# Two dense banks for the second unit's scores in a paired visit of a two-layer graph attention kernel

## The chip, the cores and the metric

The kernel runs on one core of one Trainium2 chip. The metric is the device time of one execution in microseconds (us), the median of several runs. The profile shows one more execution, instruction by instruction: TensorE's matmuls (PE) and its weight loads (PEld), VectorE (DVE), ScalarE (ACT), GpSimd (POOL), and SyncE (SP), which here issues the transfers.

## The reference, cut to what matters

There are 64 graphs of 256 nodes with 512 features, and an adjacency mask of 256 x 256 for each. Two attention layers follow each other:

```python
h = relu(layernorm(x))
x = x + attention0(h, adj)          # 4 heads of 64; masked scores, softmax, values, output product
h = relu(layernorm(x))
x = x + attention1(h, adj)          # LayerNorm with gamma and beta, 8 heads of 64; mask = adj | eye
```

In each layer q, k and v are products of h with weights. For each head the scores q k^T are scaled, masked and passed through a softmax; the probabilities weigh v; the heads together are multiplied with an output weight and added to x. Everything is fp32.

## The kernel before, in words

**Tiling.** A step works on two graphs (G = 2), so there are 32 steps. Heads are taken in pairs of two 64-row halves; a pair with its two graphs is called a *unit*. Layer 0 has the units 0 and 1, layer 1 has 0 to 3. Scores are held with keys on the partitions, so the sum over keys is a small matmul with ones.

**Dense products.** Each dense product (`project_qk`, `project_v1`, `combine`) is made of seven block products, a *set*, in the order 1, 6, 5, 2, 7, 3, 4 (the output product of layer 1 has 1, 5, 2, 6, 7, 3, 4). Products 2, 3 and 4 are accumulated into the PSUM bank that 1, 5 and 7 have left, so these banks are held between the two. One such product of the projections takes about 1.75 us on TensorE (56 passes of a set in 12.2 us). Sums of input blocks (`act_sums0`, `act_sums1`) are made on POOL ahead of a set, sums of weight blocks by `weight_sum`.

**PSUM.** Of eight banks, four are the pool `ps_sc` for scores and for the weighed values, taken in rotation. Four are `ps_mm` with the names m0 to m3; `mm_tile` takes the first bank of the list `banks` that is not held, and moves it to the end of the list.

**Visits.** Between the sets stand *visits* (`visit`). A paired visit finishes two units of an earlier attention and starts two of the next:

- `key_sums`: sums of the probabilities over keys, for both old units, into one dense bank (L961)
- `invert`: the reciprocal of the sums in two halves (L983), a check of their extremes (L986), and eight transfers by SP that spread the result (L995)
- `weigh_out`: values weighed by probabilities (L931), into two banks of `ps_sc`, copied out by ACT (L943)
- `scores` for each new unit (L875): four banks, one for each graph g and each head half e
- `mask_scores` (L899, DVE): adds the mask, reading one score bank each
- `exponentials` (L904, ACT), `key_halves` (L908, POOL), and `normalise` (L1000, POOL), which multiplies the old units' values with the spread reciprocals

With two new units there are ten tiles of the four `ps_sc` banks in one visit: two for weighed values, four for the first unit, four for the second.

**What sets the order.** Nothing is scheduled by the compiler on PE, DVE, ACT and POOL: every step is entered with a place in a period (`at`, `at_dense`, `at_set`), the entries are sorted by place, and that is the order on each engine. Period units are about the length of a set on TensorE, 7 products. In the steady part there are three paired visits in a period: at AT_X = 2.0 ahead of the v products of layer 1, at AT_Q0 = 4.64 ahead of the q and k products of layer 0, and at AT_Z = 6.36 ahead of the q and k products of layer 1. An engine works through its own order strictly, and waits at each instruction for what it needs.

**The start.** The weights of layer 1 come transposed. `weight_load(n)` loads a quarter, `weight_block` transposes one of 16 blocks on TensorE (L466) into a dense bank and copies it out in two halves (L471), on DVE or ACT. In this part `combine_rows` (L849) makes the output product of layer 0 for the first graphs in four rows, each evacuated by DVE (L854) and put through two rounds of statistics (L577, L578), POOL (L587 and around it) and ACT (L593), before `transpose_h` (L662).

Of the kernel before, what the change touches and what calls it, by code (L numbers as in the profile page):

```python
# [8 lines left out]
FP = mybir.dt.float32  # L9
# [306 lines left out]
def fast_path(  # L316
# [19 lines left out]
    nc = tc.nc  # L336
    P = 128
    B, N, D = x.shape
    DH = 64
    G = 2  # L340
    NSTEP = B // G
    NIC = N // P
# [14 lines left out]
    ps_sc = ctx.enter_context(tc.tile_pool(name="ps_sc", bufs=4, space=bass.MemoryType.PSUM))  # L357
# [4 lines left out]
    banks, held = ["m0", "m1", "m2", "m3"], set()  # L362

    def mm_tile(shape, dt=FP, hold=False):
        tag = next(b for b in banks if b not in held)
        banks.remove(tag)
        banks.append(tag)
        if hold:
            held.add(tag)
        return ps_mm.tile(shape, dt, name="mm", tag=tag)  # L370
# [82 lines left out]
    def weight_load(n):  # L453

        if n == 1:
            wr = io.tile([P, 4, D], FP, name="wr", tag="xt")
        else:
            wr = act.tile([P, 4, D], FP, name="wr", tag="v1")
        src, r0 = (w_qkv, 4 * n) if n < 3 else (w_out, 0)
        nc.sync.dma_start(wr, src[r0 * P:(r0 + 4) * P].rearrange("(r p) i -> p r i", p=P))  # L460
        return wr

    def weight_block(wr, n, c):
        pw = mm_tile([P, 4 * P])
        for r in range(4):
            nc.tensor.transpose(pw[:, r * P:(r + 1) * P], wr[:, r, c * P:(c + 1) * P], ident)  # L466
        for i in range(2):
            blk = A_OF[i, c // HC]
            dst = wqkv1[:, blk, c % HC, n, :] if n < 3 else wo1[:, blk, c % HC, :]
            copy = nc.vector.tensor_copy if i == 0 and (n > 1 or c == 0) else nc.scalar.copy  # L470
            copy(dst, pw[:, i * H1:(i + 1) * H1])  # L471


# [387 lines left out]

    units = [0]

    def scores(s, lyr, pr):
        st = S[s]
        qk = st.pop(("qk", lyr, pr))
        sc = [[ps_sc.tile([P, NIC, N], FP, name="sc") for e in range(2)] for g in range(G)]
        for g in range(G):  # L870
            for kc in range(NIC):
                for e in range(2):
                    rows = slice(e * DH, (e + 1) * DH)
                    k0 = g * N + kc * P
                    nc.tensor.matmul(  # L875
                        sc[g][e][:, kc, :], qk[rows, 1, k0:k0 + P],
                        qk[rows, 0, g * N:(g + 1) * N], start=True, stop=True,
                    )

        last = (s, lyr) == (NSTEP - 1, 1)  # L880
        if last and pr == 1:
            both = act.tile([P, 2, G, NIC, N], FP, name="p", tag="h")
            p = [both[:, e] for e in range(2)]
        elif last and pr == 3:
            p = [
                wqk0[:, 4:6].rearrange("p n c k o -> p (n c k o)").rearrange("p (g k n) -> p g k n", g=G, k=NIC),
                act.tile([P, G, NIC, N], FP, name="p", tag="v0"),
            ]
        else:
            p = [sm.tile([P, G, NIC, N], FP, name="p", bufs=4) for _ in range(2)]  # L890
        pd = sm.tile([P, 2, G, N], FP, name="pd", bufs=2)
        st["sc", lyr, pr], st["p", lyr, pr] = sc, (p, pd)
# [58 lines left out]
    def key_sums(s, lyr, prs):  # L951

        st = S[s]
        bank = mm_tile([P, 2, N])
        for i, pr in enumerate(prs):
            _, pd = st["p", lyr, pr]
            st["sums", lyr, pr] = bank[:, i]
            for g in range(G):
                for e in range(2):
                    r0 = 32 * (2 * g + e)  # L960
                    nc.tensor.matmul(  # L961
                        bank[r0:r0 + 32, i, :], ones, pd[:, e, g, :], start=True, stop=True,
                        skip_group_check=True,
                    )
# [41 lines left out]
    PERIOD, FIRST = 6.4, 6.2  # L1006
# [3 lines left out]
    def at(period, place, fn, *args):  # L1010
        events.append((period * (PERIOD if period >= 0 else FIRST) + place, len(events), fn, args))
# [15 lines left out]
    def visit(period, w, prev, cur):  # L1027

        w -= 0.0003
        s, lyr, prs = prev  # L1030
        last = (s, lyr) == (NSTEP - 1, 1)
        if prs:
            at(period, w, key_sums, s, lyr, prs)
            if prs[0] == 0 and not last:
                at(period, w, place_values, s, lyr)
            for i, pr in enumerate(prs):
                k = i if len(prs) > 1 else pr % 2
                at(period, w + 0.1 * last, invert, s, lyr, pr, k, (0,) if i and not last else (0, 1))
                if not last:
                    at(period, w, weigh_out, s, lyr, pr)  # L1040
                    at(period, w + (0.55 if len(prs) == 1 else (0.3, 0.75)[i]), normalise, s, lyr, pr)
        for i, pr in enumerate(cur[2]):
            unit = (*cur[:2], pr)
            one = len(cur[2]) == 1
            at(period, w, scores, *unit)
            at(period, w, mask_scores, *unit, 0)
            at(period, w + 1 / 7 if one else w, mask_scores, *unit, 1)
            if i == 0 and len(prs) > 1 and not last:
                at(period, w, invert, s, lyr, prs[1], 1, (1,))
            for g, place in enumerate((0.05, 0.22) if one else ((0.02, 0.03), (0.15, 0.3))[i]):  # L1050
                at(period, w + place, exponentials, *unit, g)
            for e, place in enumerate((0.23, 0.3) if one else ((0.1, 0.11), (0.35, 0.36))[i]):
                at(period, w + place, key_halves, *unit, e)

    AT_X, AT_C0, AT_Q0, AT_V0, AT_H1, AT_Z = 2.0, 4.0, 4.64, 5.64, 6.21, 6.36
    LAST_QK = 4.0
    none, L0, L1A, L1B = (NSTEP, 0, ()), (0, 1), (0, 2), (1, 3)
    for s in range(NSTEP - 1):
        visit(s, AT_X, (s + 1, 0, L0), (s, 1, L1A))
        if s < NSTEP - 2:  # L1060
            visit(s, AT_Q0, (s, 1, L1A), (s, 1, L1B))
            visit(s, AT_Z, (s, 1, L1B), (s + 2, 0, L0))

    p = NSTEP - 2
# [10 lines left out]
    visit(-2, FIRST_V0, none, (0, 0, (0,)))  # L1075
    visit(-2, FIRST_H1, (0, 0, (0,)), (0, 0, (1,)))
    visit(-2, FIRST_H1 + 0.67, (0, 0, (1,)), none)
    visit(-1, 1.53, none, (1, 0, L0))
    for s in range(NSTEP):

        p = s - 2
# [30 lines left out]
        for t in range(NT):  # L1112
            place = (FIRST_V0 + 0.14 * t - (0 if t else 0.0005), (4.31, 5.02, 5.16, 5.31)[t])[s] if s < 2 else AT_V0 + 0.14 * t
            at_dense(p, place, 0.14, project_v0, s, t)
        p = s - 1
        if s == 0:
            p -= 2.23 / FIRST
        edge = 0 if s == 0 else 1 if s == NSTEP - 1 else 2
# [12 lines left out]
        for k in range(NT):  # L1131
# [6 lines left out]
            place = ((3.6112, 3.6113, 3.7502, 3.7503)[k], 3.6 + 0.01 * k, 5.85 + 0.06 * k)[edge]  # L1138
            at(p, place, scale_row, s, NORM1[k] if edge < 2 else k)

        turn = (3.765, 3.9995, AT_H1)[edge]
        for c in range(NC):
            at(p, turn + 0.00001 * c, transpose_h, s, 1, c)
        at(p, turn + (0.001, 0.0001, 0.155)[edge], lambda s=s: act_sums0(S[s]["hT"]))
# [1 line left out]
        p = s  # L1146
        if s < NSTEP - 1:
# [3 lines left out]
            p, place = (s + 1, 1.0) if s < NSTEP - 2 else (s, LAST_QK + 2)  # L1151
# [4 lines left out]
        else:  # L1156
            p = s - 1
# [16 lines left out]
    for i in range(4):  # L1174
        at(-2, 3.01, weight_sum, nc.vector, wqk0, i)
        at(0, 0.9, weight_sum, nc.gpsimd, wo0, i)
    for n, (p, place) in enumerate(((-2, 4.0), (-2, 4.0), (-1, 0.0), (-1, 1.7))):
        at(p, place, lambda n=n: blocks.update({n: weight_load(n)}))
    at(-2, FIRST_V0 + 0.2, lambda: gamma_beta(gbr[0]))
    for i in range(16):  # L1180
        place = 3.3 - 3.93 + (1 + i) / 7 - 0.0005 if i < 6 else 0.3701 + 0.0001 * i if i < 8 else 1.6 + 0.01 * (i - 8) if i < 12 else 6.2 + 0.9995
        at(-1, place, lambda i=i: weight_block(blocks[i // 4], i // 4, i % 4))
    for i in range(4):
        at(-1, 0.1 + 0.01 * i, weight_sum, nc.vector, wqkv1[:, :, :, 0, :], i)
# [57 lines left out]
```

## Time and profile before

| what | value |
|---|---|
| median of three runs | 3425.72 us (3424.96 to 3425.89) |
| the profiled execution | 3424.34 us, span 3422.6 us |
| granted TensorE clock | 0.999 |
| PE busy | 3403.6 us, 99% of the span |
| POOL, DVE, ACT busy | 65%, 57%, 37% |
| scores, L875: matmuls | 3072 passes, 462.9 us busy |
| scores, L875: weight loads | 314.7 us busy, 151.3 us idle before them |
| one steady period (between the visits at 1483.41 and 1589.34 us) | 105.9 us |

Busy time of matmuls includes their overlap: they are pipelined, and a pass of 256 columns is shown with about 380 ns though one starts every 0.216 us. So a short stall between two passes does not show as idle time of PE. It shows as idle time ahead of a weight load (PEld), and in the distance from one matmul's start to the next. Each matmul of fp32 appears as two passes in the trace: the eight matmuls of a unit's scores are 16 passes.

### The profile page before, as it was taken

Reading aid. Unit: us, or ns where it says so; the run is one execution under the profiler, and the core shown is the slowest. Engines: PE = TensorE matmul, PEld = TensorE weight load, DVE = VectorE, ACT = ScalarE, POOL = GpSimd, SP = SyncE. Lnnn points to the kernel's source line nnn. Section 1 sums busy time; section 2 is a strip of 40 time slices with the busy share of each in tenths; the row PEclk is TensorE's granted clock in tenths of the full one; section 3 lists DMA queues with packets and bytes.
Section 4 is the critical chain, followed back from the end, with each engine's and each line's share of the span. In section 5 each row is a group of like instructions: output and inputs, shape, how many; then the busy total and the mean of one; then the engine's idle time right before and its main releaser. Section 6 shows DMA issues by size and latency. Waiting matters only on the chain.

```text
span 3422.6 us, 59964 instructions
## 1 busy us (share of the span) xinstructions
PE 3403.6 (99%) x22962; PEld 2741.9 (80%) x22962; DVE 1960.1 (57%) x3445; ACT 1253.6 (37%) x2221; POOL 2239.5 (65%) x2124
## 2 busy tenths in 40 slices
PE   9999999999999999999999999999999999999999
PEld 6878788787888878788787888888787887878877
DVE  6555655556555565555655555555556555565555
ACT  4334343333433333433434234343343433334331
POOL 6867675666766666666666576666676766667653
PEclk9999999999999999999999999999999999999999
DMA  4112111211111120111211112111111112111111
GB/s 129 42 56 59 44 43 42 58 57 50 38 54 48 55 61 27 56 46 55 61 30 55 44 55 61 35 52 42 57 59 45 43 42 58 57 52 35 55 31 45
DMA packets 168132, 174.08 MB, mean 51 GB/s; under 512 B 59672, under 2 KB 113056, under 8 KB 167840
## 3 DMA queue, kind: packets, MB, share of 16 engines
q1 hardware_dynamic: 167408, 169.78, 16.9%
q8 instruction: 184, 3.01, 0.4%
q14 instruction: 108, 0.88, 0.1%
q10 hardware_dynamic: 432, 0.40, 0.0%
HBM read 86.12 MB, written 33.62 MB: 35 GB/s over the span
## 4 chain that ended last, share of the span: by engine, by line
PE 85%; POOL 13%; issue 1%; DVE 1%; DMA 1%; SPq 0%; ACT 0%; POOLq 0%
PE mm L766 33%; PE mm L823 17%; PE sc L875 12%; PE mm L807 12%; PE sc L931 7%; POOL xt L639 4%; POOL qk L776 2%; PE mm L961 2%; PE mm L662 2%; POOL hT L412 1%; POOL hT L409 1%; POOL hT L413 1%; POOL n L569 1%; POOL r L587 1%; POOL n L572 1%
## 5 line engine op out<-in xcount | busy, mean ns | idle before, releaser
L908 POOL TENSOR_TENSOR pd<-p 128x512 f32<-128x512 f32 x383 | 478.1, 1269 | 494.1 <-ACT p L904 492.5
L766 PE MATMUL mm<-hT,wqkv 128*128 128x256 f32 x3584 | 787.4, 380 | 1.0 <-ACT wqkv L471 1.0
L766 PEld LDWEIGHTS mm<-hT,wqkv 128*128 128x128 f32 x3584 | 678.2, 190 | 103.2 <-issue 11.1
L823 PE MATMUL mm<-wo,oT 128*128 128x256 f32 x2632 | 585.6, 380 | 0.4
L823 PEld LDWEIGHTS mm<-wo,oT 128*128 128x128 f32 x2632 | 495.1, 190 | 77.1 <-POOL hT L414 11.1
L899 DVE TENSOR_TENSOR p<-sc,n 128x512 f32<-128x512 f32 x766 | 475.0, 682 | 110.5 <-PE sc L875 109.1
L983 DVE RECIPROCAL oT<-mm 128x128 f32<-128x128 f32 x376 | 345.1, 939 | 290.0 <-PE mm L961 286.3
L904 ACT ACTIVATE p<-p 128x512 f32<-128x512 f32 x766 | 443.6, 627 | 174.9 <-DVE p L899 174.5
L875 PE MATMUL sc<-qk 64*128 64x256 f32 x3072 | 462.9, 402 | 2.3
L875 PEld LDWEIGHTS sc<-qk 64*128 64x128 f32 x3072 | 314.7, 186 | 151.3 <-DVE p L899 75.9
L807 PE MATMUL mm<-wqkv,hT 128*128 128x256 f32 x1792 | 401.9, 382 | 0.0
L766 PE MATMUL mm<-hT,wqk 128*128 128x256 f32 x1792 | 399.0, 382 | 0.7 <-DVE qk L706 0.6
L943 ACT COPY oT<-sc 128x512 f32<-128x512 f32 x188 | 110.0, 585 | 762.9 <-PE sc L931 758.7
L766 PEld LDWEIGHTS mm<-hT,wqk 128*128 128x128 f32 x1792 | 338.2, 191 | 56.6 <-issue 11.3
L807 PEld LDWEIGHTS mm<-wqkv,hT 128*128 128x128 f32 x1792 | 335.5, 190 | 53.8 <-issue 10.7
L931 PE MATMUL sc<-p,v 128*32 128x256 f32 x6128 | 349.9, 379 | 0.4 <-issue 0.4
L931 PEld LDWEIGHTS sc<-p,v 128*32 128x32 f32 x6128 | 199.8, 110 | 132.2 <-issue 1.2
L1000 POOL TENSOR_TENSOR oT<-oT 128x512 f32<-128x512 f32 x188 | 239.3, 1273 | 60.3 <-DMA oT<-oT 54.0
L734 POOL TENSOR_TENSOR xt<-xt,u 128x512 f32<-128x512 f32 x183 | 229.6, 1276 | 11.4 <-DVE xt L723 9.0
L793 PE MATMUL mm<-wv,hT 128*128 128x256 f32 x1024 | 226.9, 379 | 0.0
L793 PEld LDWEIGHTS mm<-wv,hT 128*128 128x128 f32 x1024 | 194.3, 190 | 27.1 <-issue 0.6
L409 POOL TENSOR_TENSOR hT<-hT 128x512 f32<-128x512 f32 x64 | 81.7, 1277 | 185.7 <-ACT hT L666 174.6
(132 smaller groups left out, 3660.9 us busy)
## 6 DMA issues: line engine op xcount, KB each, us to landing
oT<-oT SPq DMA_DIRECT2D x1504, 32.0 KB, 1.9
xt<-in_x_dram SPq DMA_DIRECT2D x31, 1024.0 KB, 6.0
h<-in_x_dram SPq DMA_DIRECT2D x31, 1024.0 KB, 5.5
out_dram<-xt SPq DMA_DIRECT2D x31, 1024.0 KB, 4.4
ne<-row SPq DMA_DIRECT2D x30, 256.0 KB, 4.8
ad<-in_adj_dram SPq DMA_DIRECT2D x32, 128.0 KB, 9.1
wr<-in_L_gnn_w_qkv_dram SPq DMA_DIRECT2D x3, 1024.0 KB, 8.7
h<-in_x_dram SPq DMA_DIRECT2D x4, 256.0 KB, 3.9
```

The source lines that it names most:

```text
L734: (nc.vector if last else nc.gpsimd).tensor_tensor(r, r, u, ALU.add)
L766: nc.tensor.matmul(bank[:, k, :], w[:, wa, c, k, a * P:(a + 1) * P], st["hT"][:, ba, c, :], start=first and (k, c) == (0, 0), stop=(k, c) ...
L793: nc.tensor.matmul(bank, st["hT"][:, b0 + t // NIC * step, c % HC, i:i + P], wv0[:, c, :], start=(c == 0), stop=(c == NC - 1),)
L807: nc.tensor.matmul(bank[:, t, :], st["hT"][:, ba, c, t * P:(t + 1) * P], wqkv1[:, wa, c, 2, :], start=first and (t, c) == (0, 0), stop=(t, ...
L823: nc.tensor.matmul(bank[:, t, :], oT[:, ba, c, t * P:(t + 1) * P], w[:, wa, c, :], start=first and (t, c) == (0, 0), stop=(t, c) == (NIC - ...
L875: nc.tensor.matmul(sc[g][e][:, kc, :], qk[rows, 1, k0:k0 + P], qk[rows, 0, g * N:(g + 1) * N], start=True, stop=True,)
L899: nc.vector.tensor_tensor(p[e][:, g], sc[e], neg[:, :, g, :], ALU.add)
L904: nc.scalar.activation(p[e][:, g], p[e][:, g], AF.Exp, scale=SCALE)
L908: nc.gpsimd.tensor_tensor(pd[:, e], p[e][:, :, 0, :], p[e][:, :, 1, :], ALU.add)
L931: nc.tensor.matmul(po[r0:r0 + 32, g, :], st[f"v{lyr}"][:, g * NIC + kc, pr * P + r0:pr * P + r0 + 32], p[r0 // DH][:, g, kc, :], start=(kc ...
L983: nc.vector.reciprocal(inv[:, k * P:(k + 1) * P], sums[:, k * P:(k + 1) * P])
L1000: nc.gpsimd.tensor_tensor(dst, dst, invb, ALU.mult)
```

## The change

There are three edits.

First, in a paired visit the second unit's scores of the first graph (g = 0) go into two banks of `ps_mm`, taken by `mm_tile`, in place of two of `ps_sc`. The bank that holds the sums of the keys in this visit is remembered in `sums_bank`, and moved to the end of the list, so that later dense products take it last. A visit then has eight tiles of `ps_sc`: the second unit's second graph (g = 1) takes the two banks of the first unit's first graph.

Second, on DVE the second half of the second old unit's reciprocal, with its check and its transfers, moves from the place behind the first new unit's masks to a place between the second new unit's two pairs of masks.

Third, in the start: weight blocks 7 to 11 get other places (block 7 behind a v product, 8 to 11 one behind each row of `combine_rows`), the load of the last quarter is entered at 1.1 in place of 1.7, the copies of five blocks go to ACT instead of DVE, the visit for step 1 becomes two visits of one unit each, on either side of the transposes of step 0's h, and the late place of the second mask is kept for step 0 alone.

```diff
-            copy = nc.vector.tensor_copy if i == 0 and (n > 1 or c == 0) else nc.scalar.copy
+            copy = nc.vector.tensor_copy if i == 0 and (n > 2 or (n, c) == (0, 0)) else nc.scalar.copy
...
-    units = [0]
+    units, sums_bank = [0], []
-    def scores(s, lyr, pr):
+    def scores(s, lyr, pr, second):
         st = S[s]
         qk = st.pop(("qk", lyr, pr))
-        sc = [[ps_sc.tile([P, NIC, N], FP, name="sc") for e in range(2)] for g in range(G)]
+        sc = [
+            [mm_tile([P, NIC, N]) if second and g == 0 else ps_sc.tile([P, NIC, N], FP, name="sc") for e in range(2)]
+            for g in range(G)
+        ]
+        if second and sums_bank:
+            tag = sums_bank.pop()
+            banks.remove(tag)
+            banks.append(tag)
...
         bank = mm_tile([P, 2, N])
+        sums_bank[:] = [banks[-1]] if len(prs) > 1 else []
...
-            one = len(cur[2]) == 1
-            at(period, w, scores, *unit)
+            one = cur[:2] == (0, 0)
+            at(period, w, scores, *unit, i == 1)
             at(period, w, mask_scores, *unit, 0)
+            if i == 1 and len(prs) > 1 and not last:
+                at(period, w, invert, s, lyr, prs[1], 1, (1,))
             at(period, w + 1 / 7 if one else w, mask_scores, *unit, 1)
-            if i == 0 and len(prs) > 1 and not last:
-                at(period, w, invert, s, lyr, prs[1], 1, (1,))
...
-    visit(-1, 1.53, none, (1, 0, L0))
+    visit(-1, 1.53, none, (1, 0, (0,)))
+    visit(-1, 1.54, none, (1, 0, (1,)))
...
-        turn = (3.765, 3.9995, AT_H1)[edge]
+        turn = (3.763, 3.9995, AT_H1)[edge]
...
-    for n, (p, place) in enumerate(((-2, 4.0), (-2, 4.0), (-1, 0.0), (-1, 1.7))):
+    for n, (p, place) in enumerate(((-2, 4.0), (-2, 4.0), (-1, 0.0), (-1, 1.1))):
...
-        place = 3.3 - 3.93 + (1 + i) / 7 - 0.0005 if i < 6 else 0.3701 + 0.0001 * i if i < 8 else 1.6 + 0.01 * (i - 8) if i < 12 else 6.2 + 0.9995
+        place = (
+            *(3.3 - 3.93 + (1 + k) / 7 - 0.0005 for k in range(7)), 0.5205,
+            *(0.53 + 0.14 * (k + 1) - 0.0005 for k in range(4)), *(FIRST + 0.9995 for k in range(4)),
+        )[i]
```

## The prediction

> **What bounds the kernel now.** I read the page first: busy times, then the costliest groups; then the waits, and last the timeline of single visits.
>
> ```profile
> span 3422.6 us, 59964 instructions
> PE 3403.6 (99%) x22962; PEld 2741.9 (80%) x22962; DVE 1960.1 (57%) x3445; ACT 1253.6 (37%) x2221; POOL 2239.5 (65%) x2124
> ...
> L899 DVE TENSOR_TENSOR p<-sc,n 128x512 f32<-128x512 f32 x766 | 475.0, 682 | 110.5 <-PE sc L875 109.1
> ...
> L875 PE MATMUL sc<-qk 64*128 64x256 f32 x3072 | 462.9, 402 | 2.3
> L875 PEld LDWEIGHTS sc<-qk 64*128 64x128 f32 x3072 | 314.7, 186 | 151.3 <-DVE p L899 75.9 <-issue 40.3 <-POOL hT L413 13.0
> ```
>
> TensorE is busy 99% of the span, so only what shortens its own stream shortens the kernel. But its matmuls overlap, and a short stall hides inside "busy". The weight loads beside it (PEld) show it: one group, the scores of L875, has its loads idle for 151.3 us, half of that until a mask addition (L899, DVE) had read a score bank. The list of waits says the same:
>
> ```profile
> PEld sc L875 <- DVE p L899: 75.9, 254, 0.4
> ```
>
> 254 such waits over the paired visits is 2.7 each. One visit of the steady part, weight loads, then matmuls, then DVE:
>
> ```profile
> 1525.54 1.60 PEld L875 LDWEIGHTS sc<-qk 64*128 64x128 f32 x16 [0.41 <-issue]
> 1527.45 0.29 PEld L875 LDWEIGHTS sc<-qk 64*128 64x128 f32 x2 [0.31 <-DVE p L899]
> 1528.05 0.89 PEld L875 LDWEIGHTS sc<-qk 64*128 64x128 f32 x8 [0.30 <-DVE p L899]
> 1529.24 0.73 PEld L875 LDWEIGHTS sc<-qk 64*128 64x128 f32 x6 [0.30 <-DVE p L899]
> ```
> ```profile
> 1525.54 4.83 PE L875 MATMUL sc<-qk 64*128 64x256 f32 x32
> 1530.30 12.35 PE L766 MATMUL mm<-hT,wqk 128*128 128x256 f32 x56
> ```
> ```profile
> 1526.70 2.48 DVE L899 TENSOR_TENSOR p<-sc,n 128x512 f32<-128x512 f32 x4 [1.14 <-PE sc L875]
> 1529.11 0.95 DVE L983 RECIPROCAL oT<-mm 128x128 f32<-128x128 f32 x1
> ...
> 1530.43 2.48 DVE L899 TENSOR_TENSOR p<-sc,n 128x512 f32<-128x512 f32 x4
> ```
>
> The first unit's 16 passes load without a break. The second unit restarts at 1527.45, 1528.05 and 1529.24, each just after a mask ended: its four banks are the first unit's, and masks come at 0.60 us a bank. The stage costs 1530.30 - 1525.54 = 4.76 us. What would it cost unstalled? A visit of one unit shows it:
>
> ```profile
> 29.27 2.00 PE L875 MATMUL sc<-qk 64*128 64x256 f32 x16
> 31.20 1.99 PE L793 MATMUL mm<-wv,hT 128*128 128x256 f32 x8
> ```
>
> 16 passes take 31.20 - 29.27 = 1.93 us, entering and leaving the form included. Passes go in pairs (two row halves at once) every 0.216 us (inside the visit: 1526.290, 1526.506, 1526.721), so 16 more cost 8 x 0.216 = 1.73, and 32 cost 3.66. A paired visit loses 1.10 us, and 1.17 where it takes 4.83.
>
> **What the Trainium skill says.** "PSUM — Partial Sum Buffer", Specifications: eight banks a partition; four serve scores and four the dense products here, so banks can only be borrowed. "Perfetto Trace Analysis", Matmuls: independent groups should rotate through different banks, so that evacuation overlaps the next group. The trace agrees: 0.30 us idle at each restart where the second unit reuses the first one's banks, none inside the first. "TensorE: Matmul & The Clock Gate", The mechanism: matmuls start and end in program order. So a late bank holds all that follows, and any new wait of a dense product would too.
>
> **The change, part by part.** Times count from a visit's first score pass, V.
>
> 1. *Banks.* The second unit's g=0 takes two dense banks. Their last readers stand ahead of this visit's reciprocals on DVE, or ended on ACT before, so they are free. The second unit's g=1 then takes the score banks of the first unit's g=0. Unstalled it wants them at V + 0.31 + 11 x 0.216 = V+2.69, its weights some 0.19 us earlier, V+2.50. The masks freed them at 1527.45 and 1528.05, V+1.91 and V+2.51. So in the visits of 4.76 us the stall goes almost wholly. In the 4.83 us kind the second bank comes at V+2.58 (1558.27 after 1555.69), 0.08 late; I charge 0.1. Counting all 94 paired visits with an earlier pair (three in each of 30 rounds, one more in the last, three at the end) by their own durations gives 105.6 us; less 0.1 x 30, **102.6 us off TensorE's path**.
>
> 2. *The new wait.* The dense banks are now also freed by masks. The order of the set is 1, 6, 5, 2, 7, 3, 4; product 1 gets the fourth, untouched bank, products 6 and 5 the borrowed ones, 7 the bank of the sums. Product 6 starts at V+3.66+1.73 = V+5.4, 5 at V+7.1. With the masks of the second unit's g=0 ahead of the reciprocal, DVE has them done at V+3.57+0.60 = 4.2 and 4.8: 1.2 us or more to spare, cost nothing. Without that move the reciprocal (0.95), the check (0.43) and the accumulator read would stand in front, and they would end at 5.5 and 6.1, too late for 6. The sums' bank is free at about V+6.1, product 7 wants it at V+10.6. Behind product 6 on TensorE's queue is the whole set; nobody waits if it doesn't.
>
> 3. *Reciprocal later.* The second reciprocal half moves behind two masks, 1.2 us, and with it eight SP transfers (0.62 us each to issue, 1.9 to land) and one multiplication L1000 on POOL. No work is added: the second unit's last mask ends at V+7.4 as before. In the visit at 1555.69 L1000 would go from 1567.24 to about 1568.4, and the four sums of oT1 behind it on POOL from 1573.5 to 1574.7. The output product needing the second of them starts 3 x 1.75 us into the stage that began at 1572.71, or 1.17 earlier now: 1576.8 against 1572.2. Cost nothing, 4 us of cover. At most visits a DMA wait on POOL grows by about 1 us, in POOL's 35% idle time.
>
> 4. *Does the rest keep up?* After the visit at 1525.54 DVE idles 1.21 us for a dense product (1534.13), so its work moves up with TensorE; the chain from it over POOL (L587) and ACT (L593, done 1548.51) ends 0.88 us ahead of the transposes at 1549.39, and keeps that. A round is 105.9 us, with DVE at 60, POOL at 70: neither becomes the bound at 102.6.
>
> 5. *Weight blocks and the first rounds.* Same transposes, other places; five 0.42 us copies go from DVE to ACT. Two TensorE stalls there go, 0.8 us (two blocks in a row at 62.51, waiting for L710) and 1.1 us (L766 at 86.43, for L471), and 1.0 from the visit at 76.87: 4.83 against two single visits of 1.93 around the transposes. New risks: block 8 wants its rows at about 65.7 (their packets ended near 63, from 57.69); the transposes at 80.1 want rows scaled by about 79.5, since the four products of L849, spread out by blocks, still feed DVE at its own rate. On SP the output weights' load is issued before the next graph's h. Between -1 and +3 us; I take a gain of 2.5.
>
> Sum: 102.6 + 2.5 = 105.1. The profiled execution took 3424.34 us (span 3422.6), so 3319.2; the median of the runs is 1.4 higher, **3320.7 us**, 3.1% less.
>
> **The rivals.**
> - *A: as above*, 76%: 3312 to 3330, by part 5's bounds and up to 0.1 us a visit on the restart.
> - *B: the second half still restarts.* The bank needed at V+2.50 comes at V+2.51; if the wait costs a whole restart (0.31 instead of 0.216) plus lateness at each of two banks, 0.3 us a visit stay: 28 us, about 3349, or 3330 to 3360. For it: the margins are zero in 62 visits and negative in 30. Against: inside 1525.54 a load 0.015 us late shifted nothing. 15%.
> - *C: given back downstream.* TensorE arrives 1.1 us earlier at the transposes, whose rows have 0.88 us of cover, if one link stays fixed in time (ACT's exponentials move up only 0.8 us). Once a round up to 1.1 us, or two such waits: 3360 to 3415. Against: the chain's DVE part waited for TensorE. 5%.
> - *D: slower.* Product 6 waits for a borrowed bank. It decides when the mask ends past V+5.4, and turns the sum when it is over 1.1 us later still, V+6.5, against V+4.2 worked out. At 0.3 us beyond that in each visit it gives 3425.7 + 28 = 3454. It needs DVE 2.3 us late. 3%.
> - *E: nothing happens*, if the dense banks were never free at the visit; the wait would only change its name. 1%.
>
> **How the numbers follow.** About 0.2% (7 us) is what a measurement of this kernel can tell from no change. A, B and C are faster: 0.96; E is the same: 0.01; slower 0.03. The likeliest is A, 3320.7. The range runs from 3312 (A's lower end, all of the 3 us of part 5 and no restart) to 3348, to take in the larger part of B.
>
> **What would show it.** Right: the wait of L875's loads for the masks falls from 75.9 us to under 10; a paired visit lasts 3.66 to 3.8 us from its first score pass to the next product; the next products have no new idle loads; a round takes 102.4 to 102.7 us; the additions of L899 now read mm as well as sc; POOL's wait for DMA at L1000 rises from 54.0 us, at no cost. B would leave restarts in the second unit's last eight passes. C would show loads of L662 or L823 idle for ACT or POOL. D would show loads of the second product in a set idle for the mask additions. I am wrong if the visits shorten and the round doesn't.

## The result and the profile after

| | us |
|---|---|
| before, median of four runs | 3425.48 (3424.96 to 3425.89) |
| after, median | 3316.51 (3316.21 to 3317.53) |
| ratio | 0.9682 (0.9666 to 0.9699) |
| the profiled execution after | 3317.53, span 3315.7 |
| predicted | 3320.7 (3312 to 3348) |

The kernel is 109.0 us faster, 3.2%. The page of the kernel after, its busy times and the groups of the scores (now L883) and of the mask additions (now L907; the last line is from the list of groups by form):

```profile
PE 3298.3 (99%) x22962; PEld 2717.9 (82%) x22962; DVE 1959.3 (59%) x3440; ACT 1260.5 (38%) x2226; POOL 2244.7 (68%) x2124
...
L907 DVE TENSOR_TENSOR p<-sc,n 128x512 f32<-128x512 f32 x579 | 363.6, 684 | 111.2 <-PE sc L883 109.8
...
L883 PE MATMUL sc<-qk 64*128 64x256 f32 x2320 | 292.6, 385 | 0.0
L883 PEld LDWEIGHTS sc<-qk 64*128 64x128 f32 x2320 | 218.7, 186 | 58.8 <-issue 38.8
```
```profile
L907 DVE TENSOR_TENSOR p<-mm,n 128x512 f32<-128x512 f32 x187 | 119.6, 681 | 0.0
L883 PE MATMUL mm<-qk 64*128 64x256 f32 x752 | 96.8, 376 | 0.0
L883 PEld LDWEIGHTS mm<-qk 64*128 64x128 f32 x752 | 72.8, 187 | 8.3
```

The scores now stand in two groups: 752 passes, eight in each of the 94 paired visits, write mm. The idle time ahead of the loads is 58.8 + 8.3 = 67.1 us; it was 151.3. The mask additions, which ended 75.9 us of it, are gone from the list. So is a line of the kernel before that stood for the same thing:

```profile
PEld sc L875 <- POOL hT L413: 13.0, 29, 0.4
```

These 29 loads start 0.11 to 0.12 us after a mask addition has ended, at V+2.04 (V is the start of the visit's first score pass). With them and two more called "issue" there are 285 restarts, three in each of the 95 paired visits of the kernel before, where the prediction read 254, or 2.7 each. The largest part of what is left is "issue", 0.41 us once a visit where the form of the matmuls changes. TensorE issues as many passes as before, 22962; only their spacing changed.

One visit, weight loads and then DVE, of the kind shown before (it starts at 1479.36):

```profile
1479.36 1.60 PEld L883 LDWEIGHTS sc<-qk 64*128 64x128 f32 x16 [0.41 <-issue]
1480.98 0.84 PEld L883 LDWEIGHTS mm<-qk 64*128 64x128 f32 x8
1481.84 0.84 PEld L883 LDWEIGHTS sc<-qk 64*128 64x128 f32 x8
1483.02 11.95 PEld L766 LDWEIGHTS mm<-hT,wqk 128*128 128x128 f32 x56 [0.33 <-issue]
```
```profile
1480.53 2.48 DVE L907 TENSOR_TENSOR p<-sc,n 128x512 f32<-128x512 f32 x4 [1.14 <-PE sc L883]
1482.93 1.28 DVE L907 TENSOR_TENSOR p<-mm,n 128x512 f32<-128x512 f32 x2
...
1484.12 0.95 DVE L992 RECIPROCAL oT<-mm 128x128 f32<-128x128 f32 x1
...
1485.45 1.28 DVE L907 TENSOR_TENSOR p<-sc,n 128x512 f32<-128x512 f32 x2
```

The 32 passes load in one stream, and from the first to the next product it is 1483.02 - 1479.36 = 3.66 us (3.65 in the mean of all 94 visits). The 56 loads of the next set follow without a break, so no new wait stands behind it. DVE does what it did, in the new order. A round went from 105.9 to 102.55 us.

### The profile page after: what moved, and what is told of

The parts are those of the page before. It is cut to its first block, busy times and chain, and to the rows that moved or that the text cites. A ratio compares the mean times of both kernels' runs of the same rounds, so it can differ in the third digit from the quotient of the medians.

```text
span 3315.7 us, 60001 instructions
## 1 busy us (share of the span) xinstructions
PE 3298.3 (99%) x22962; PEld 2717.9 (82%) x22962; DVE 1959.3 (59%) x3440; ACT 1260.5 (38%) x2226; POOL 2244.7 (68%) x2124
## 4 chain that ended last, share of the span: by engine, by line
PE 99%; DMA 1%; DVE 0%; SPq 0%; issue 0%; DVEq 0%
PE mm L766 35%; PE mm L823 17%; PE mm L807 12%; PE sc L939 10%; PE sc L883 8%; PE mm L793 7%; PE mm L662 3%; PE mm L970 3%; PE mm L883 2%; PE mm L550 0%; PE mm L849 0%; DMA h<-in_x_dram 0%; PE mm L466 0%; DMA wv<-in_L_gnn_Wv_dram 0%; SPq L431 0%
## 5 line engine op out<-in xcount | busy, mean ns | idle before, releaser
L766 PE MATMUL mm<-hT,wqkv 128*128 128x256 f32 x3584 | 787.4, 380 | 0.0
L766 PEld LDWEIGHTS mm<-hT,wqkv 128*128 128x128 f32 x3584 | 678.2, 190 | 102.2 <-issue 11.4
L823 PE MATMUL mm<-wo,oT 128*128 128x256 f32 x2632 | 585.7, 380 | 0.4
L823 PEld LDWEIGHTS mm<-wo,oT 128*128 128x128 f32 x2632 | 495.0, 190 | 77.3 <-POOL hT L414 11.2
L907 DVE TENSOR_TENSOR p<-sc,n 128x512 f32<-128x512 f32 x579 | 363.6, 684 | 111.2 <-PE sc L883 109.8
L766 PE MATMUL mm<-hT,wqk 128*128 128x256 f32 x1792 | 398.7, 382 | 1.6 <-DVE qk L706 1.3
L766 PEld LDWEIGHTS mm<-hT,wqk 128*128 128x128 f32 x1792 | 338.2, 191 | 57.6 <-issue 12.0
L883 PE MATMUL sc<-qk 64*128 64x256 f32 x2320 | 292.6, 385 | 0.0
L883 PEld LDWEIGHTS sc<-qk 64*128 64x128 f32 x2320 | 218.7, 186 | 58.8 <-issue 38.8
L593 ACT ACTIVATE h<-h,mr,r 128x512 f32<-128x512 f32 x252 | 188.2, 809 | 16.3 <-POOL mr L589 16.3
```

Source lines behind the costliest of these rows:

```text
L766: nc.tensor.matmul(bank[:, k, :], w[:, wa, c, k, a * P:(a + 1) * P], st["hT"][:, ba, c, :], start=first and (k, c) == (0, 0), stop=(k, c) ...
L823: nc.tensor.matmul(bank[:, t, :], oT[:, ba, c, t * P:(t + 1) * P], w[:, wa, c, :], start=first and (t, c) == (0, 0), stop=(t, c) == (NIC - ...
L883: nc.tensor.matmul(sc[g][e][:, kc, :], qk[rows, 1, k0:k0 + P], qk[rows, 0, g * N:(g + 1) * N], start=True, stop=True,)
L907: nc.vector.tensor_tensor(p[e][:, g], sc[e], neg[:, :, g, :], ALU.add)
```

## The experiments

The first four share one chip and its runs of the kernel before (median 3425.07 us), the last three another (3425.08). The kernel after has no runs on these two chips, so the ratios to the kernel before are what can be compared.

**Borrowed banks with the masks in the old order.**

```diff
-            if i == 1 and len(prs) > 1 and not last:
-                at(period, w, invert, s, lyr, prs[1], 1, (1,))
             at(period, w + 1 / 7 if one else w, mask_scores, *unit, 1)
+            if i == 0 and len(prs) > 1 and not last:
+                at(period, w, invert, s, lyr, prs[1], 1, (1,))
```

> The changed kernel with the second half of the reciprocal back in its old place, ahead of the second unit's masks; the borrowed banks stay. My theory (the borrowed bank holds product 6 until its mask is done): the mask of the second unit's first bank then ends at about V+5.6 instead of V+4.3, product 6 wants its bank at V+5.2, so each of some 91 visits loses about 0.35 us: 3345 to 3353 us, with idle weight loads of the second product of a set, put down to the mask additions. Rival (the order of the masks is idle, the banks alone carry the gain): 3316 to 3319. Rival (a visit's gain depends on both in full): 3400 or more.

Measured: 3346.87 us, ratio 0.9772 (0.9755 to 0.9788): 30 us of the 109 are lost. The timeline of a visit that starts at 1449.94, DVE and the next set's loads:

```profile
1453.51 0.95 DVE L992 RECIPROCAL oT<-mm 128x128 f32<-128x128 f32 x1
1453.59 1.59 PEld L807 LDWEIGHTS mm<-wqkv,hT 128*128 128x128 f32 x8 [0.33 <-issue]
...
1454.84 1.28 DVE L907 TENSOR_TENSOR p<-mm,n 128x512 f32<-128x512 f32 x2
1455.58 1.59 PEld L807 LDWEIGHTS mm<-wqkv,hT 128*128 128x128 f32 x8 [0.39 <-DVE p L907]
```

The scores still run in 3.65 us; the stall has moved to the ninth pass of the set, where product 6 takes a bank whose mask now stands behind the reciprocal. Its loads stand idle 0.39 us, and a round has 103.52 us, 0.97 more, 0.32 a visit. So the order of the masks is worth 30 us, but only together with the banks:

**The masks' order without the banks.** The same lines moved as in the change, in the kernel before.

> The kernel before with the masks of the second unit's first graph moved ahead of the reciprocal's second half, and no borrowed banks. My theory: the second unit restarts behind the FIRST unit's masks, which don't move, so 3424 to 3427 us, the same as before, with the same 254 waits of about 0.30 us. Rival (earlier masks free banks earlier, and carry a part of the gain): 3420 or less.

Measured: 3424.74 us, ratio 0.9999 (0.9990 to 1.0007). The list of waits is what it was:

```profile
PEld sc L875 <- DVE p L899: 76.1, 254, 0.4
```

The second unit restarts behind the first unit's masks, and those don't move.

**The sums' bank left in its turn.**

```diff
-        if second and sums_bank:
+        if False:
```

> The changed kernel without the step that moves the bank of the key sums to the end of the list: product 6 then gets that bank, and waits for the check behind the second reciprocal half, which ends at about V+6.1 where the product wants the bank at V+5.2. My theory: 0.8 to 0.95 us in each of some 92 visits, 3390 to 3404 us, most of the gain gone. Rival (something in the visit is later anyway and hides it): 3316 to 3330.

Measured: 3414.79 us, ratio 0.9970 (0.9959 to 0.9982). Nearly the whole gain goes, 98 us, and more than expected. A visit that starts at 1475.20:

```profile
1480.95 0.43 DVE L995 CUSTOM_DVE_ANT_0 mm<-mm,oT 128x256 f32<-128x256 f32 x1
1481.30 0.14 DVE L995 DVE_READ_ACCUMULATOR2_ANT extremes<- 128x1 f32 x1
...
1481.49 5.04 PEld L807 LDWEIGHTS mm<-wqkv,hT 128*128 128x128 f32 x24 [1.04 <-DVE extremes L995]
```

The accumulator read ends at V+6.24 and the load starts at V+6.29, where the expectation had V+6.1. In the visits ahead of L766 the list of waits names POOL instead (69.5 us, 61 times), but there too the load that waits starts 0.11 us after the accumulator read, in nearly every visit. A round grows by 2.92 us, 0.97 a visit, and the last visit, whose reciprocals are entered later, stops TensorE once for 5.0 us. Without the three lines that put one name at the end of a list, nine tenths of the gain are gone.

**One borrowed bank.**

```diff
-            [mm_tile([P, NIC, N]) if second and g == 0 else ps_sc.tile([P, NIC, N], FP, name="sc") for e in range(2)]
+            [mm_tile([P, NIC, N]) if second and g == 0 and e == 0 else ps_sc.tile([P, NIC, N], FP, name="sc") for e in range(2)]
```

> The changed kernel with one borrowed bank instead of two (g=0, e=0 alone); the other three of the second unit stay in the score banks. My theory (each score bank of the second unit waits for the mask addition of the one it takes over): restarts of about 0.2 us at the second bank (free at V+1.9, wanted at V+1.6) and 0.3 us at the last (free at V+3.1, wanted at V+2.7): 0.5 us a visit, 3358 to 3370 us. Rival (the restart at V+1.9 alone): 3330 to 3340. Rival (no gain below two banks): 3400 or more.

Measured: 3367.12 us, ratio 0.9830 (0.9814 to 0.9847); a visit lasts 4.19 us in the mean, 0.54 more. Its list of waits has one of the mask additions again, for the scores:

```profile
PEld sc L883 <- DVE p L907: 23.2, 94, 0.3
```

This is the restart at the last bank. The one at the second bank leaves no idle time in the list, since the loads of the other head half go on meanwhile: in the visit at 1499.48 its first load starts at 1501.39, 0.29 us behind that of the other half. One bank gives about half, two give all: each bank of the second unit has its own date.

**The reciprocal's second half behind all masks.**

```diff
-            if i == 1 and len(prs) > 1 and not last:
-                at(period, w, invert, s, lyr, prs[1], 1, (1,))
             at(period, w + 1 / 7 if one else w, mask_scores, *unit, 1)
+            if i == 1 and len(prs) > 1 and not last:
+                at(period, w, invert, s, lyr, prs[1], 1, (1,))
```

> The changed kernel with the second half of the reciprocal, its check and its transfers behind all masks of the visit, 1.2 us later still. My theory (this chain has cover: product 7 wants the bank of the sums at V+10.6, and POOL's sums for the output product have some 3 us left): 3315.5 to 3317.5 us, unchanged, while POOL's wait for transfers ahead of the multiplication (184 us in the changed kernel) grows by up to 1.2 us a visit. Rival (the chain over SP and POOL is on the path): 3330 or more.

Measured: 3316.69 us, ratio 0.9684 (0.9671 to 0.9697), the kernel after. POOL's wait for the spread reciprocals went up in two steps; the kernel before, after, and this one:

```profile
POOL oT L1000 <- DMA oT<-oT: 54.0, 46, 2.4
```
```profile
POOL oT L1009 <- DMA oT<-oT: 184.2, 99, 3.6
```
```profile
POOL oT L1009 <- DMA oT<-oT: 273.4, 99, 3.8
```

130 us and then 89 us more of waiting, and no effect on the time: POOL has that room in each round.

**Without the edits of the start.** The six edits of the start are undone; the visits are as changed.

> The changed kernel with all edits of the start undone (places of the weight blocks and of the last quarter's load, copies on ACT, one paired visit for step 1); the paired visits of the steady part stay as changed. The prediction's 2.5 us for the start would give 3319.0 us. The profiles of before and after show the first steady visit at 106.15 and 105.19 us, so 1.0 us is my theory now: 3317 to 3318. Rival (the start edits give nothing): 3316.0 to 3316.9.

Measured: 3317.93 us, ratio 0.9687 (0.9673 to 0.9700), against 3316.69 for the experiment before it on the same chip, which times as the kernel after: 1.2 us, about as large as the spread of a kernel's own runs, so this is a size, not a proof. The traces agree with it. They have to be read from the first scores on, since these start at 28.95 to 30.80 us in the nine profiles, and a gap of 0.5 to 1.3 us ahead of the first steady visit ("issue") differs as well. From the first scores to that visit, without the excess of this gap, it is 76.3 us before, 75.0 here and 73.8 after. The five other profiles that have the edits of the start give 73.8 to 74.1 by the same reading. So the start gives 2.2 to 2.5 us in all, and 1.3 without its own edits: step 1's paired visit takes 3.65 instead of 4.83 us with borrowed banks alone. The two visits of 1.93 us that replace it take 3.86, so by these lengths its split no longer pays by itself; no run tests the split alone.

**Another order in the output product of layer 0.** This one follows from a stall that the profiles of both kernels show: product 4 waits for the evacuation of product 7.

```diff
-    SETC0 = (1, 6, 5, 2, 7, 3, 4)
+    SETC0 = (1, 6, 7, 5, 2, 4, 3)
...
+    SUM_U0 = {5: (3,), 3: (1,), 4: (2,)}
...
-        for k in (SUM_U_LAST if last else SUM_U).get(n, ()):
+        for k in (SUM_U_LAST if last else SUM_U0 if lyr == 0 else SUM_U).get(n, ()):
```

> The changed kernel with another order of the seven block products of layer 0's output product: 1, 6, 7, 5, 2, 4, 3 instead of 1, 6, 5, 2, 7, 3, 4, and the addition of u to the last quarter after product 5 instead of 7. In each of 29 or 30 rounds product 4 waits 0.18 us for the evacuation of product 7, which there has only one product between (0.392 instead of 0.216 from one start to the next). With two products between, theory: the wait goes, 5.2 us less, 3310 to 3312.5. Rival (the wait moves to another product, or DVE is late with two evacuations): 3316 or more.

Measured: 3309.21 us, ratio 0.9661 (0.9648 to 0.9675); the runs, 3308.55 to 3310.27, lie below all of the two others on this chip. The set's weight loads in the kernel after, then here:

```profile
1468.41 5.05 PEld L823 LDWEIGHTS mm<-wo,oT 128*128 128x128 f32 x24
1473.04 0.69 DVE L723 TENSOR_TENSOR xt<-mm,xt 128x512 f32<-128x512 f32 x1 [0.17 <-PE mm L823]
...
1473.85 0.73 PEld L823 LDWEIGHTS mm<-wo,oT 128*128 128x128 f32 x4 [0.39 <-POOL hT L414]
```
```profile
1465.56 5.91 PEld L824 LDWEIGHTS mm<-wo,oT 128*128 128x128 f32 x28
...
1469.52 1.27 POOL L414 TENSOR_TENSOR hT<-hT 128x512 f32<-128x512 f32 x1
```

The break ahead of the last four loads is gone. The trace puts it down to POOL's sum (L414), but the load starts 0.12 us after DVE's evacuation of product 7 has ended (L723). And in the new order product 4 starts at 1469.99, before that sum ends at 1470.79: POOL had no part in it. The gain is 7.3 to 7.5 us where 5.2 were expected. The set went from 6.08 to 5.83 us in all 30 rounds: 0.25, not 0.18. The rest is the pass behind the one that waits, which I had left out: it starts 0.29 us after it instead of 0.216. This version beats both kernels.

## Why the prediction was right, and where its sizes were off

The likeliest case came, 4.2 us below its number; 3.6 of them are in step 1. By the prediction's steps:

1. *Banks*: right. By the durations of the 94 visits in the two traces, 106.2 us came off; the sum was 105.6 less a charge of 3.0 (for 30 visits of the longer kind; there are 32). The charge is the term that was mis-sized. In the kind of visit that took 4.83 us the last bank does come late: its first load starts at V+2.58 (1510.986 after 1508.407), 0.09 us behind the place it would have had. But the passes keep their places, 1511.103 and 1511.319. This wait costs nothing. Rival B rested on the same margin and had no part. The other 0.6 us is the visit's length, 3.654 and not 3.66, 94 times.
2. *The new wait*: right, and shown by undoing each of its two conditions. With the masks behind the reciprocal product 6 stalls by 0.32 us a visit; with the sums' bank next in turn, by 0.97. D's mechanism exists, but its date was never reached in the steady part. Once, behind the last visit, whose reciprocals are entered later, the set waits 0.26 us for the bank of the sums; that costs 0.12 us.
3. *Reciprocal later*: right. The transfers wait longer, and twice that delay still cost nothing.
4. *The rest keeps up*: right. The round has 102.55 us, where 102.4 to 102.7 was expected, with DVE and POOL as busy per round as before (60.4 and 70.2 us). C did not happen: L662 has one idle load of 0.3 us in the whole run, and the waits of L823 that the list puts down to POOL are as before (11.2 us after 11.1).
5. *The start*: 2.5 us predicted, 2.2 to 2.5 found from the first scores on, of which 1.3 comes from the borrowed banks and not from the edits of the start. Of the two stalls named, that of two blocks in a row kept 0.5 of its 0.8 us: the same evacuation (L710) now holds the v product (0.68 us from start to start at 62.31). The profiled execution shows only 1.0 us at the first steady visit, because its opening was 0.8 us and the gap ahead of that visit 0.7 us longer than in the profile of before.

106.2 and 2.2 to 2.5 make 108.4 to 108.7, and the medians differ by 109.0; what is left is inside the spread of the runs, 0.9 us before and 1.3 after.

## What to carry to other kernels

Busy time of the matmuls hid the stalls here: TensorE was 99% busy before and after. Read them from the idle time of the weight loads and from the distance between starts, and price the stage from a place in the same trace where it runs unstalled. Buffers borrowed from another stage are worth only as much as the next date at which that stage wants them back: write down for each bank when it is freed and when it is wanted, and order both the list that hands them out and the work that frees them by these dates. A step on another engine may then move at no cost, as the reciprocal did here by 1.2 and by 2.4 us, while those two dates stay apart.

## What the runs showed that I had not expected

A wait of TensorE inside a set costs more than the time by which the waiting pass starts late. The pass behind it is late as well: it starts 0.29 to 0.32 us after the waiting one instead of 0.216. In the order of the output product this made 0.25 us out of 0.18. Counted from the weight load that waits, the sum is simple. It is worked out from the distances between starts. In the four profiles of the kernel before, the kernel after, the masks in the old order and the sums' bank in its turn, such loads start 0.23 to 1.15 us behind the place they have without a wait, and each wait costs that lateness less 0.11 to 0.12 us: 0.12 us for a load that is 0.23 late, 0.25 for 0.36, 0.39 for 0.50, 1.04 for 1.15. The load that was 0.09 us late in the visits above cost nothing, which fits. So about the first 0.11 us of lateness were free here, and the rest was paid in full; between 0.09 and 0.23 us no run has a case.
